# Eight buffers for the places of a group's rows, and block 1's experts on four column quarters with weights fetched early and the last choice's parts overlapped

## The chip, the cores and the metric

The kernel runs on one core of a Trainium2 chip. The metric is the device time of one execution in microseconds, the median of ten executions. The profiled execution is another one of the same program; its span goes from the first instruction to the last.

The engines are TensorE (PE, with its weight loads shown as PEld), VectorE (DVE), ScalarE (ACT), GpSimd (POOL) and SyncE (SP). SP, ACT and POOL issue DMA transfers; sixteen DMA engines carry them. A matmul of f32 stands in the profile as two MATMUL instructions, each with a weight load of its own; they are called passes here.

## The reference

The input is 32 images of 128 channels, 56x56 pixels, in f32. Two blocks follow each other. Block 0 is a depthwise 7x7 convolution, a layer norm over the channels and a mixture of eight experts, two for each of the 100,352 tokens, with a capacity for each expert. Block 1 takes the tokens of each image (3136) through an attention in which each token only attends within its own channels, head by head, and then through experts that choose tokens:

```python
logits = jnp.einsum('bsd,ed->bse', x, gate_w) + gate_b
probs = jax.nn.softmax(logits, axis=1)
vals, idx = jax.lax.top_k(probs.transpose(0, 2, 1), K)
...
pooled = jnp.einsum('bked,bke->bed', gathered, topv)
h = jnp.concatenate([pooled.transpose(1, 0, 2), ones], axis=-1)
h = jax.nn.gelu(jnp.einsum('ebd,edh->ebh', h, weight1), approximate=False)
h = jnp.concatenate([h, ones], axis=-1)
out = jnp.einsum('ebh,eho->ebo', h, weight2)
...
weighted = jnp.einsum('beo,bke->bkeo', out, topv).reshape(Bn, K * E, O)
outputs = outputs.at[jnp.arange(Bn)[:, None], flat_idx].add(weighted)
```

So each of the 64 experts sees one pooled row of 128 channels for each of the 32 images, takes it to 512 features (weight1, whose last row is a bias), through a Gelu and back to 128 channels (weight2, also with a bias row). The result goes back to the chosen tokens with the weights they were chosen with.

## The kernel before

**Stages.** One after the other: the convolution on PE (to `conv_d` in DRAM); routing of block 0's tokens; the choice of who keeps a place; the scatter of rows to their experts; block 0's experts; block 1's attention with the choices of its experts; block 1's experts; the output. Instructions are put in an order by the tile framework, which also inserts the waits and may move an instruction ahead of others on its engine; where `InOrder` wraps an engine (line 161, which all its instructions carry in the profile), the order of the text holds.

**Scatter (lines 659 to 810).** 112 groups of 896 tokens, seven tiles of 128 tokens each. In each turn of the loop `places(g)` has DVE write the row numbers of a group into `rd` (4 buffers, the pool's number), `rows(g)` builds the rows `xs` (6 buffers), and `send(g)`, two turns after `places`, has POOL issue seven indirect DMAs (line 697), which read `rd` and `xs`. A buffer of `rd` is free for DVE when the DMAs of the group four before have landed.

**Attention.** A loop over 784 tiles of 128 tokens, software-pipelined by hand. The 128x2048 tiles `s` (5 buffers) and `ev` (3) carry the scores and the weighted values of one tile each, 8 KB a partition. The pool `at` holds them and all else of the loop. Work of a group of seven tiles hangs at given places of the loop, and after every second image `choose(pr)` runs for a pair of images: the eight largest of 3136 for each expert and image (DVE), the exponentials (ACT), the chosen weights `pb`, stored to `mk_d` (SP), and then ten parts. A part transposes `pb` in tiles (PE, `cm`), scales them (ACT, `mT`), multiplies them with the normed tokens `u` (PE, `acc`) and adds the sum to `pT` (DVE). `choose` is a generator; each `yield` gives way to other work until the next half step. For the last pair there is no other work left.

**Block 1's experts (lines 1422 to 1486).** These open when the attention's pools are closed. `hbr` (biases of weight1) is fetched and turned, `pT` is turned to `pTb` (channels x experts x images, four matmuls of 512 columns, two PSUM buffers). Then 16 steps of four experts each. A step fetches `fw1` (1 MB, SP), `fw2` (four DMAs of 256 KB in rows of 512 bytes, ACT, line 1455) and the bias rows `fw2b` (SP); all three have 3 buffers. The products have weight1 as the stationary operand and 32 columns, one for each image, as the moving one, 16 matmuls `p_fh` a step (line 1463); DVE adds the bias, ACT applies the Gelu, and 16 matmuls `p_fo` (line 1480) with the 32 columns stationary and 128 columns of weight2 moving give 32 rows (images) by 4x128. DVE adds the bias row into `so`. After the last step `so` is stored to `fo_d` in one DMA (1 MB, line 1485) and read back as `outF` with the experts on the partitions (1 MB in rows of 512 bytes, line 1486), both on SP.

**Output (lines 1488 to 1500).** For each image SP fetches the chosen weights `mk` (784 KB, and 12 KB of `al`) and the tokens `to` (1568 KB), PE multiplies `outF` with `mk` in seven chunks of 448, DVE adds, and ACT stores 1568 KB. All tiles have 2 buffers.

Of the kernel before, what the change touches and what calls it, by code (L numbers as in the profile page):

```python
# [8 lines left out]
F32 = mybir.dt.float32  # L9
I32 = mybir.dt.int32  # L10
U32 = mybir.dt.uint32
AF = mybir.ActivationFunctionType
# [5 lines left out]
P = 128  # L18
# [7 lines left out]
def conv_attn_hybrid_kernel(  # L26
# [632 lines left out]
    with tc.tile_pool(name="sc_c", bufs=1) as cc, tc.tile_pool(  # L659
# [89 lines left out]
        def places(g):  # L749
# [5 lines left out]
            rds[g] = sc.tile([P, GJ], I32, name="rd")  # L755
# [169 lines left out]
    FAR = -3.0e38  # L925
    with tc.tile_pool(name="at_c", bufs=1) as cc, tc.tile_pool(
# [19 lines left out]
        wpr = at.tile([C, C], F32, name="wpr", tag="s", bufs=5)  # L946
# [3 lines left out]
        wpT = at.tile([C, C], F32, name="wpT", tag="ev", bufs=3)  # L950
# [142 lines left out]
        def offsets(n):  # L1093

            s = ss_[n] = at.tile(sh, F32, name="s", bufs=5)
# [17 lines left out]
        def values(n):  # L1113
            ev = evs[n] = at.tile(sh, F32, name="ev", bufs=3)
            kv = kvs[n - n % 2][:, n % 2]
            ve.tensor_tensor(ev, ss_[n], over_queries(kv[:, 1]), ALU.mult)
# [173 lines left out]
        def choose(pr):  # L1290
# [21 lines left out]
            yield  # L1312
            for im in range(2):
                e = slice(im * E2, (im + 1) * E2)
                parts = [(gl, *s[1:]) for gl in range(GPP) for s in tile_parts(gl) if s[0] == im]
                px = 0
                for gi, (gl, j0, j1, p) in enumerate(parts):
                    u, r = us[pr * GPP + gl]
                    pn, nj = p.stop - p.start, j1 - j0
                    ps = atp.tile([P, GJ, E2], F32, name="cm", tag="tp", bufs=3)  # L1320
                    for j in range(nj):
                        pe.transpose(
                            ps[:pn, j, :], pb[e, px + j * pn : px + (j + 1) * pn], ident[e, e]
                        )
                    px += nj * pn
                    yield
                    yield
                    mT = at.tile([P, GJ, E2], F32, name="mT", bufs=1)
                    if p.start:
                        sc.copy(mT[p, :nj], ps[:pn, :nj])  # L1330
                    for j in range(nj):
                        sc.activation(
                            mT[p, j], mT[p, j] if p.start else ps[p, j], AF.Copy,
                            scale=r[p, j0 + j : j0 + j + 1],
                        )
                    yield
                    yield
# [193 lines left out]
```

## Time and profile before

| | |
|---|---|
| median of ten runs | 9583.01 us (9570.92 to 9588.28) |
| profiled execution | 9579.16 us, span 9577.4 us, mean granted clock of PE 0.941 |
| busy: PE, DVE, ACT, POOL | 8686.7 (91%), 6480.8 (68%), 5266.6 (55%), 6772.9 us (71%) |
| DMA | 849.94 MB, mean 89 GB/s |

Stages by their place in the span: convolution to about 700 us, routing to 1050, keeping to 1320, scatter to 2330, block 0's experts to 4400, attention with its choices to 9018, block 1's experts to 9198, output to 9577.

In the lines below, a group of instructions is given as line, engine, operation, tile written and tiles read, shape, count, then busy time and the mean of one in ns, then the idle time before them and what ended it. A line of a window gives the busy time and count of each engine in a stretch of the span, the granted clock of PE as a share of full speed, the share in which the 16 DMA engines were busy, and GB/s. A line of the chain gives a start, a duration and what the time went to. Busy time of PE includes time in which a matmul is in the array at a lower clock.

### The profile page before, as it was taken

Reading aid. Unit: us, or ns where it says so; the run is one execution under the profiler, and the core shown is the slowest. Engines: PE = TensorE matmul, PEld = TensorE weight load, DVE = VectorE, ACT = ScalarE, POOL = GpSimd, SP = SyncE. Lnnn points to the kernel's source line nnn. Section 1 sums busy time; section 2 is a strip of 40 time slices with the busy share of each in tenths; the row PEclk is TensorE's granted clock in tenths of the full one; section 3 lists DMA queues with packets and bytes.
Section 4 is the critical chain, followed back from the end, with each engine's and each line's share of the span. In section 5 each row is a group of like instructions: output and inputs, shape, how many; then the busy total and the mean of one; then the engine's idle time right before and its main releaser. Section 6 shows DMA issues by size and latency. Waiting matters only on the chain. (4 is left out here: it accounts for less than half of the span.)

```text
span 9577.4 us, 165805 instructions
## 1 busy us (share of the span) xinstructions
PE 8686.7 (91%) x62536; PEld 7094.3 (74%) x62536; DVE 6480.8 (68%) x10965; ACT 5266.6 (55%) x13385; POOL 6772.9 (71%) x4884
## 2 busy tenths in 40 slices
PE   9999467776999999997999999999999999999888
PEld 4449445554766766666888998998988898898853
DVE  1127888885222222225999999999999999999423
ACT  1116633333333333335888888888888888888400
POOL 0002147776787777787999999999999999999300
PEclk9999789998999999999999999999999999999765
DMA  9995247775444444442000000000000000000389
GB/s 207 215 199 144 64 115 210 208 209 160 74 66 65 67 70 69 70 69 32 24 31 31 31 31 27 28 27 31 31 31 31 31 24 31 31 31 26 95 280 333
DMA packets 1019570, 849.94 MB, mean 89 GB/s; under 512 B 525876, under 2 KB 912247, under 8 KB 999250
## 3 DMA queue, kind: packets, MB, share of 16 engines
q1 hardware_dynamic: 464018, 479.57, 17.9%
q0 software_dynamic: 177664, 188.81, 11.4%
q10 hardware_dynamic: 377088, 170.96, 6.6%
q8 instruction: 495, 8.11, 0.4%
q14 instruction: 305, 2.50, 0.1%
HBM read 486.34 MB, written 353.64 MB: 88 GB/s over the span
## 5 line engine op out<-in xcount | busy, mean ns | idle before, releaser
L161 POOL TENSOR_TENSOR s<-s,q 128x2048 f32<-128x2048 f32 x784 | 3597.6, 4599 | 137.8 <-DVE s L161 106.7
L161 ACT ACTIVATE s<-s 128x2048 f32<-128x2048 f32 x784 | 1500.6, 1914 | 685.4 <-POOL s L161 682.5
L161 POOL DMA_INDIRECT t_d<-ys,xe x992 | 1530.7, 1543 | 412.0 <-issue 229.9
L161 DVE TENSOR_TENSOR s<-kv,c 128x2048 f32<-128x2048 f32 x784 | 1788.6, 2281 | 7.9 <-POOL c L161 7.6
L161 DVE TENSOR_TENSOR ev<-s,kv 128x2048 f32<-128x2048 f32 x784 | 1785.7, 2278 | 2.3 <-ACT s L161 2.2
L161 PE MATMUL sm<-ident,ev 128*128 128x128 f32 x12544 | 1534.3, 277 | 45.7 <-DVE ev L161 45.7
L161 PE MATMUL sm<-ident,s 128*128 128x128 f32 x12544 | 1525.2, 275 | 8.1 <-ACT s L161 8.1
L161 PEld LDWEIGHTS sm<-ident,ev 128*128 128x128 f32 x12544 | 1439.3, 144 | 93.2 <-DVE ev L161 50.8
L161 PEld LDWEIGHTS sm<-ident,s 128*128 128x128 f32 x12544 | 1403.1, 143 | 20.6 <-ACT s L161 8.5
L888 ACT ACTIVATE hT<-ph,b1t 128x512 f32<-128x512 f32 (+1 forms) x992 | 679.3, 685 | 1237.8 <-PE ph L884 1222.1
L899 DVE TENSOR_TENSOR ys<-py,b2t 128x512 f32<-128x512 f32 (+1 forms) x248 | 171.5, 691 | 1529.2 <-PE py L894 1427.4
L894 PEld LDWEIGHTS py<-w,hT 128*128 128x128 f32 x7936 | 958.0, 192 | 201.9 <-issue 91.4
L884 PE MATMUL ph<-xeT,w 128*128 128x512 f32 (+1 forms) x1984 | 921.6, 597 | 70.5 <-DVE xeT L880 70.5
L894 PE MATMUL py<-w,hT 128*128 128x128 f32 x7936 | 982.0, 277 | 0.1
L697 POOL DMA_INDIRECT xb_d<-xs,rd x784 | 766.2, 977 | 240.2 <-issue 203.2
L241 PE MATMUL cps<-xin,br 56*64 56x448 f32 x7168 | 686.1, 541 | 12.7 <-DVE br L235 11.0
L884 PEld LDWEIGHTS ph<-xeT,w 128*128 128x128 f32 x1984 | 348.8, 191 | 392.7 <-issue 292.8
L161 PE MATMUL pa<-rw,ct 128*128 128x256 f32 x1568 | 425.6, 416 | 202.4 <-DVE xs L161 202.4
L241 PEld LDWEIGHTS cps<-xin,br 56*64 56x64 f32 x7168 | 300.1, 133 | 398.1 <-issue 395.5
L161 PEld LDWEIGHTS pa<-rw,ct 128*128 128x128 f32 x1568 | 302.5, 205 | 335.0 <-DVE xs L161 247.1
L287 POOL MEMSET code<- 128x64 f32 x1 | 0.2, 151 | 695.2 <-DMA conv_d<-ot 695.2
L161 PE MATMUL kv<-wq,zT 128*128 128x256 f32 x1568 | 417.7, 390 | 54.4 <-DVE ev L161 54.1
(327 smaller groups left out, 13471.4 us busy)
## 6 DMA issues: line engine op xcount, KB each, us to landing
ct<-conv_d SPq DMA_DIRECT2D x192, 448.0 KB
xin<-in_x_dram SPq DMA_DIRECT2D x256, 196.0 KB
conv_d<-ot ACTq DMA_DIRECT2D x512, 98.0 KB
t_d<-xs ACTq DMA_DIRECT2D x112, 448.0 KB
tr<-t_d SPq DMA_DIRECT2D x112, 448.0 KB
to<-t_d SPq DMA_DIRECT2D x32, 1568.0 KB
out_dram<-oo ACTq DMA_DIRECT2D x32, 1568.0 KB
xg<-in_x_dram SPq DMA_DIRECT2D x96, 448.0 KB
```

The source lines that it names most:

```text
L161: r = getattr(self.engine, name)(*a, **k)
L241: nc.tensor.matmul(pss[r][b * HP : (b + 1) * HP], br[rows, kw, :], xi[rows, b * NB : (b + 1) * NB, kw : kw + W], start=(kw == 0), stop=(kw ...
L287: nc.gpsimd.memset(code, -1.0)
L697: s = nc.gpsimd.indirect_dma_start(out=xb_d, out_offset=bass.IndirectOffsetOnAxis(ap=idx, axis=0), in_=row, in_offset=None, bounds_check=R ...
L884: nc.tensor.matmul(ph[:, :, :rows], w1[:, f * P : (f + 1) * P], xT[:, :, :rows], start=True, stop=True,)
L888: nc.scalar.activation(hT[:, f, :, :rows], ph[:, :, :rows], AF.Gelu, bias=b1t[:, f : f + 1])
L894: nc.tensor.matmul(py[:rows, j, :], hT[:, f, j, :rows], w2[:, f, :], start=(f == 0), stop=(f == NF - 1),)
L899: nc.vector.tensor_tensor(ys[:rows], py[:rows], across(b2t, SB)[:rows], ALU.add)
```

## The change

**Places.** `rd` gets 8 buffers instead of 4.

**Pools.** A pool `big` is opened before the attention's pools and stays open to the end. The tiles `s` (5) and `ev` (3), and the two setup tiles that shared their buffers, move from `at` to `big`.

**Weights.** `fetch(i)` loads both weights of a step of four experts into these buffers: `fw1` into those of `s` (5), `fw2` into those of `ev` (3), each in one DMA of 1 MB on SP, and `fw2` with four consecutive rows of weight2 on a partition (2 KB in one piece). The first three steps are fetched in the loop's turn `NT + 4`, four turns after the last tile entered it and ahead of the last choice; the others inside the loop over steps.

**Last choice.** For the last pair of images the parts run in `in_turn_parts`: the next part's transposes are issued ahead of this part's sum, the parts of one image add up in PSUM (a `kv` buffer), and DVE copies the sum to `pT` once an image; `mT` takes the two buffers of `oT`. For other pairs nothing changes but that the code is cut into functions (`part_turned` is the scaling and `part_sum` the product, both as before).

**Experts.** The step's 32 columns of each expert become the stationary operand and weight1 the moving one, 512 columns; the four experts of a step stand on four column quarters of PE (`tile_position=(0, q * N)`), so that one PSUM bank holds 4x32 rows by 512. ACT copies it to SBUF, four transposes turn it back (each reads every fourth column, which fits the new order of weight2), DVE adds the bias while it empties PSUM, and the Gelu follows. The second product runs on column quarters as well, 16 matmuls of 128 columns, and its result and `so` have 128 rows (expert of the step, image). The bias rows of all steps are fetched once (`ob`, four DMAs). ACT stores each step's `so` to `fo_d`, and `outF` is read back in four DMAs of eight images each, on ACT's queue.

```diff
-            rds[g] = sc.tile([P, GJ], I32, name="rd")
+            rds[g] = sc.tile([P, GJ], I32, name="rd", bufs=8)
...
+    Q = 4
+    NS = E2 // Q
+    assert N * Q == P and 2 * NS <= 2 * E2
+
+    largest = ExitStack()
+    big = largest.enter_context(tc.tile_pool(name="big", bufs=1))
+    fw1s, fw2s = {}, {}
+
+    def fetch(i):
+
+        e = slice(i * Q, (i + 1) * Q)
+        fw1s[i] = big.tile([C, Q, FF2], F32, name="fw1", tag="s", bufs=5)
+        nc.sync.dma_start(fw1s[i], weight1[e, :C, :].rearrange("e c f -> c e f"))
+        fw2s[i] = big.tile([P, Q, NF2, C], F32, name="fw2", tag="ev", bufs=3)
+        nc.sync.dma_start(fw2s[i], weight2[e, :FF2, :].rearrange("e (p f) o -> p e f o", f=NF2))
...
-        wpr = at.tile([C, C], F32, name="wpr", tag="s", bufs=5)
+        wpr = big.tile([C, C], F32, name="wpr", tag="s", bufs=5)
...
-            s = ss_[n] = at.tile(sh, F32, name="s", bufs=5)
+            s = ss_[n] = big.tile(sh, F32, name="s", bufs=5)
...
-            ev = evs[n] = at.tile(sh, F32, name="ev", bufs=3)
+            ev = evs[n] = big.tile(sh, F32, name="ev", bufs=3)
...
+            if pr == N // 2 - 1:
+                yield from in_turn_parts(pr, pb, parts)
+                return
...
+        def part_turn(pb, part):
+            im, gl, j0, j1, p, px = part
+            e, pn = slice(im * E2, (im + 1) * E2), p.stop - p.start
+            ps = atp.tile([P, GJ, E2], F32, name="cm", tag="tp", bufs=3)
+            for j in range(j1 - j0):
+                pe.transpose(
+                    ps[:pn, j, :], pb[e, px + j * pn : px + (j + 1) * pn], ident[e, e]
+                )
+            return ps
...
+        def in_turn_parts(pr, pb, parts):
+
+
+            ahead = part_turn(pb, parts[0])
+            for i, part in enumerate(parts):
+                im, px = part[0], part[-1]
+                if px == 0:
+                    ps = atp.tile([P, E2], F32, name="acc", tag="kv", bufs=3)
+                mT = part_turned(pr, ahead, part, "oT", 2)
+                if i + 1 < len(parts):
+                    ahead = part_turn(pb, parts[i + 1])
+                done = i + 1 == len(parts) or parts[i + 1][0] != im
+                part_sum(pr, ps, mT, part, px == 0, done)
+                if done:
+                    ve.tensor_copy(pT[:, :, 2 * pr + im], ps)
+                yield
...
+            if k == NT + 4:
+                for i in range(3):
+                    fetch(i)
...
-            nc.tensor.transpose(ps[:, f, :], rows[:, f * P : (f + 1) * P], ident[:E2, :E2])
+            nc.tensor.transpose(ps[:, f, :], rows[:, f::NF2], ident[:E2, :E2])
...
+        ob = cc.tile([P, NS, C], F32, name="ob")
+        for q in range(Q):
+            nc.sync.dma_start(
+                ob[q * N : (q + 1) * N],
+                weight2[q::Q, FF2, :].partition_broadcast(N),
+            )
...
+        so = cc.tile([P, NS, C], F32, name="so")
+        for i in range(NS):
+            if i not in fw1s:
+                fetch(i)
+            w1, w2 = fw1s.pop(i), fw2s.pop(i)
+            ph = fps.tile([P, FF2], F32, name="p_fh", bufs=2)
             for q in range(Q):
-                nc.scalar.dma_start(
-                    w2[:, q], weight2[e0 + q, :FF2, :].rearrange("(f p) o -> p f o", p=P)
-                )
-            w2b = fp.tile([N, Q, C], F32, name="fw2b")
-            nc.sync.dma_start(w2b, weight2[e0 : e0 + Q, FF2, :].partition_broadcast(N))
-            ph = fps.tile([P, Q * NF2, N], F32, name="p_fh")
-            for q in range(Q):
-                for f in range(NF2):
+                nc.tensor.matmul(
+                    ph[q * N : (q + 1) * N], pTb[:, i * Q + q, :], w1[:, q, :],
+                    start=True, stop=True, tile_position=(0, q * N), skip_group_check=True,
+                )
+            h = fp.tile([P, FF2], F32, name="fh")
+            nc.scalar.copy(h, ph)
+            pt = fps.tile([P, NF2, P], F32, name="p_ft", tag="p_t", bufs=2)
+            for f in range(NF2):
+                nc.tensor.transpose(pt[:, f, :], h[:, f::NF2], ident)
+            hT = fp.tile([P, NF2, P], F32, name="fhT")
+            nc.vector.tensor_tensor(
+                hT.rearrange("p f (q n) -> p f q n", q=Q),
+                pt.rearrange("p f (q n) -> p f q n", q=Q),
+                hb[:, :, i * Q : (i + 1) * Q].unsqueeze(3).to_broadcast([P, NF2, Q, N]),
+                ALU.add,
+            )
+            nc.scalar.activation(hT, hT, AF.Gelu)
+            po = fps.tile([P, C], F32, name="p_fo", bufs=1)
+            for f in range(NF2):
+                for q in range(Q):
                     nc.tensor.matmul(
-                        ph[:, q * NF2 + f, :], w1[:, q, f * P : (f + 1) * P], pTb[:, e0 + q, :],
-                        start=True, stop=True,
+                        po[q * N : (q + 1) * N], hT[:, f, q * N : (q + 1) * N], w2[:, q, f, :],
+                        start=(f == 0), stop=(f == NF2 - 1), tile_position=(0, q * N),
+                        skip_group_check=True,
                     )
-            hT = fp.tile([P, Q * NF2, N], F32, name="fhT")
-            nc.vector.tensor_tensor(
-                hT.rearrange("p (q f) n -> p q f n", f=NF2),
-                ph.rearrange("p (q f) n -> p q f n", f=NF2),
-                hb[:, :, e0 : e0 + Q].rearrange("p f q -> p q f").unsqueeze(3).to_broadcast(
-                    [P, Q, NF2, N]
-                ),
-                ALU.add,
-            )
-            nc.scalar.activation(hT, hT, AF.Gelu)
-            po = fps.tile([N, Q, C], F32, name="p_fo")
-            for q in range(Q):
-                for f in range(NF2):
-                    nc.tensor.matmul(
-                        po[:, q, :], hT[:, q * NF2 + f, :], w2[:, q, f, :],
-                        start=(f == 0), stop=(f == NF2 - 1),
-                    )
-            nc.vector.tensor_tensor(so[:, e0 : e0 + Q, :], po, w2b, ALU.add)
-        nc.sync.dma_start(fo_d, so)
-        nc.sync.dma_start(outF[:E2], fo_d.rearrange("n e c -> e n c"))
+            nc.vector.tensor_tensor(so[:, i, :], po, ob[:, i, :], ALU.add)
+            nc.scalar.dma_start(
+                fo_d.rearrange("n (s q) c -> s q n c", q=Q)[i], so[:, i, :]
+            )
+        for n in range(0, N, N // 4):
+            nc.scalar.dma_start(
+                outF[:E2, n : n + N // 4, :], fo_d[n : n + N // 4].rearrange("n e c -> e n c")
+            )
```

## Prediction

> **What bounds the kernel now.** I read the page first, then the windows of the two places that the change touches, then the chain of waits and the groups by line there. On the page, POOL, DVE and PE are busy in turn over most of the span; a share of the whole says little here, so each stage is read for itself.
>
> The scatter stage (some 1325 to 2330 us), where the places are used, by groups of instructions on POOL:
>
> ```profile
> L697 POOL DMA_INDIRECT xb_d<-xs,rd x469 | 458.6, 978 | 142.9 <-issue 121.0 <-DVE xs L161 16.7 <-DMA xb_d<-xs,rd 4.0
> ```
>
> This is a window of 600 us: 458.6 us busy and 142.9 us between, 601.5 us together. POOL issues one indirect DMA each 1.28 us (0.98 and a gap of 0.30) without a hole. The waits of the same window name the one the new buffers concern:
>
> ```profile
> DVE rd L161 <- DMA xb_d<-xs,rd: 48.8, 34, 3.9
> ```
>
> DVE stands 48.8 us for a free place buffer, but in this window it is busy 80 to 85 us in each 100, and POOL never runs dry.
>
> The end of the kernel, as windows (stretch; PE, PEld, DVE, ACT, POOL busy with counts; granted clock; DMA share; GB/s). The rows are the last choice's sums, the start of the experts, the experts, the way of their output through memory, and the output loop:
>
> ```profile
> 8982.30:9018.00 35.70, 30.67 (x150) 27.81 (x150) 2.46 (x10) 11.54 (x51) 0.00 (x0) 0.50 0.11 46
> 9018.00:9028.00 10.00, 8.09 (x14) 3.28 (x14) 6.33 (x8) 0.00 (x0) 0.00 (x0) 0.50 0.93 279
> 9028.00:9181.00 153.00, 150.49 (x1025) 143.96 (x1023) 22.39 (x33) 11.35 (x17) 0.00 (x0) 0.75 0.82 231
> 9181.00:9198.40 17.40, 0.01 (x1) 0.01 (x1) 0.23 (x1) 0.00 (x0) 0.00 (x0) 0.63 0.91 213
> 9198.40:9577.40 379.00, 343.93 (x448) 145.83 (x448) 134.22 (x224) 0.00 (x0) 0.00 (x0) 0.50 0.94 327
> ```
>
> In the experts PE is busy 150.5 of 153 us at a clock of 0.75, while the DMA moves 231 GB/s: PE sets that stage. The output loop is the reverse: 327 GB/s at a DMA share of 0.94, so its 379 us are the transfers' and nothing in the change shortens them. The groups of the experts show what PE does:
>
> ```profile
> L1463 PE MATMUL p_fh<-pTb,fw 128*128 128x32 f32 x512 | 81.2, 331 | 0.0
> L1480 PE MATMUL p_fo<-fw,fhT 128*32 128x128 f32 x512 | 70.2, 309 | 2.0 <-ACT fhT L1476 2.0
> ```
>
> Each of the 16 steps of four experts costs (81.2 + 70.2) / 16 = 9.5 us of PE, in 64 passes (a matmul of f32 is two). The first kind streams 32 columns past a fresh 128x128 load: 159 ns a pass, most of it loading. The chain that ended last agrees, and shows the way through memory after it:
>
> ```profile
> 9122.78 16.37 PE p_fh L1463 x96
> 9139.16 13.21 PE p_fo L1480 x96
> ...
> 9181.26 6.47 DMA fo_d<-so
> 9187.74 10.61 DMA outF<-fo_d
> ```
>
> And before the experts, the last choice's parts, one after the other:
>
> ```profile
> 8987.00 0.95 PE cm L161 x7
> 8987.98 0.05 issue
> 8988.03 0.32 ACT mT L161
> 8988.35 0.04 issue
> 8988.40 3.25 PE acc L161 x14
> ```
>
> **The change part by part.** The profiled execution has a span of 9577.4 us; the median of the ten runs is 9583.0, so 5.6 us are added at the end.
>
> **Eight place buffers: 0 us.** The wait of 48.8 us per 600 moves off DVE, but POOL's 784 issues at 1.276 us stay. The work that hides it is POOL's own queue; had POOL holes, the most to win would be its gaps not put down to issue, 16.7 + 4.0 us per 600, 35 us in the stage. Those gaps are, however, the same 0.30 us that every issue has, so I take 0. A loss would need DVE running ahead to hurt POOL, whose beat did not change while DVE waited or worked: bounds -3 to +3.
>
> **The last choice: -4.5 us.** Ten parts now take PE 30.67 us of 35.7 at half clock; the rest is PE waiting some 0.4 us a part for the first ACT scaling (4.9 us of idle before the sums, released by ACT). With the next part's transposes placed ahead of the sum, only the first wait stays. The scalings are seven at 0.22 us, 1.54 us a part, under the 4.2 us of PE. The ten DVE additions become two copies; they were off the path (0.27 us each). Bounds: 0, and -17 if the clock rises: the same parts took 0.65 + 1.77 us instead of 1.0 + 3.25 at clock 1.00 near 8950 us. The clock stayed at 0.50 at 86% busy here, so I take it held.
>
> **Weights of three steps early: priced with the experts.** Six transfers of 1.05 MB wait for the last s and ev tiles, free near 8950 us. The DMA is nearly idle there (0.06 share, then 0.00), and 6.3 MB at 343 GB/s (the output loop from 9300 to 9500 us) are 18 us, done before the choice ends at 9018. On SP, the last stores of t2 and al (8957 to 8968) and the 1.6 MB of chosen weights (8982) are queued behind them, none needed before the output loop. Without that cover the 18 us would come back.
>
> **The experts, by step: 163.3 to 106 us.** The start stays: 10.2 us from the last sum (9017.9) to the first product (9028.1), for pT's turn, the biases and four copies. Then, of each step:
> - First product, 4 matmuls of 512 columns, two passes each. A 512-column pass took 0.94 us at half clock (p_b, x4 in 3.75) and 0.46 at full (the experts of block 0, 921.6 us by 1984). If four column quarters run at once: 1.9 or 0.9 us. In the first convolution four 64x64 quarters do: 7168 passes of 535 ns in 686 us, 96 ns each.
> - Copy by ACT 0.59 (u<-p_u, same shape). Four transposes back, 8 passes of 0.226 us at half clock (sm, 16 in 3.62) or 0.119 at full: 1.8 or 0.95. This work is new. Bias 0.69, Gelu 0.63, as now.
> - Second product, 16 matmuls of 128 columns, four at a time: 8 pass times, 1.8 or 0.95. Its addition 0.35 (between 0.28 for 128x64 and 0.42 for 128x256). Handovers at some 0.08, 0.5.
>
> PE: 5.5 us a step at half clock, 2.8 at full, instead of 9.5. The chain from copy to addition, if steps do not overlap: 6.4 or 4.7 us. ACT loses the 64 issues of w2 (median 0.62 us, with waits that held its Gelu up for 86 us); they go to SP as 16 of about 0.4 us, beside 16 of w1 as now, and SP loses 16 bias rows for 4 at the start. ACT gains a store a step, 0.4 us, which waits for the step's last addition with the next step's copy behind it: it can only make the chain hold. DMA: 2.10 MB a step at 328 GB/s (325 and 330 in the two stretches where PE drew it hardest, 9028 to 9047 and 9105 to 9123) is 6.4 us. The three limits lie close together, and none near 9.5.
>
> From the end of the choice: the three early steps begin at 10.2, the first second product ends near 19 and frees the first of three w2 buffers; SP has waited there with the DMA idle for about 10 us. 24 transfers of 3.2 us follow without a hole: 77 us, to 96; the last product and addition 2 us, 98. The first images' loads, up to 4.8 MB, take between 0 and 15 us of this, as now (two were there before the output began). Half of it: 106 us. Bounds: 93 (343 GB/s, no loads between) and 10.2 + 16 x 7.5 = 130 (nothing overlaps, a hole of 1 us a step for the buffer's return).
>
> Two pages of the Trainium skill speak against the new form. TensorEngine Tiling, Tiling Modes, says that a change of tiling mode drains TensorE; each step of the new form changes twice, from quarters to whole for the transposes and back, where today's never does. No row shows a drain's length, and the convolution kept one mode. SBUF — State Buffer, Specifications, says that reads want at least two hits in a 16-byte line; the transposes read h at every fourth f32, one hit a line. By contiguous rows a load is 0.143 us; were it twice that, the eight of a step would add 1.1 us, 18 over the stage where the chain binds, and the sum would be 9531. The time goes by the contiguous row, the nearest.
>
> **Output of the experts: 17.1 to 8.4 us.** One store of 1 MB (6.5 us) becomes sixteen, of which only the last is after the addition; the read (10.6 us, while a 1.6 MB load ran beside it) becomes four. The tail of the old read ran near 175 GB/s, 6.0 us for 1.05 MB; with 2.4 for the last small store: 8.4. SP no longer stands at the store, and loads pass it. Bounds: 17 (the new store lands as slowly) and 5 (only the first quarter is waited for).
>
> **Sum.** 9577.4 - 0 - 4.5 - (163.3 - 106) - (17.1 - 8.4) = 9506.9 us of span; with 5.6: 9512.5, say 9513.
>
> **The rivals.**
> *The steps run as chains.* ACT's issue keeps the order and half clock stays: 130 us instead of 106, 9537. For it: four engine handovers a step and short bursts, as where the clock stands at 0.50 today. Against: now two or three steps are held together (x96), and two buffers of each tile remain.
> *DMA alone, at a risen clock.* 93 us, 13 less in the choice than taken (-12 instead of -4.5 is enough): 9513 - 13 - 7.5 - 1.5 = 9491. For it: the choice without holes. Against: the experts held 0.75 even at 98% busy.
> *The quarters do not run side by side* (the other side). Then a step has 8 passes of 512 columns, 8 transposes, and 32 passes of 128. At a clock of 0.75: 5.1 + 1.2 + 4.9 = 11.2 us, 189 us with the start, and 9513 + 83 = 9596; at half clock 16.6 us, above 9650. It decides from 10.4 us a step on: (163.3 + 4.5 + 8.7 - 10.2) / 16. For it: here quarters have 128 rows and 32 columns, a form that no row shows. Against: the convolution's 96 ns.
> *It does not do what it says.* The weight transfers stay behind the pool's release, or a single queue paces the stage like now: 9583 less 4.5 and 8.7, 9570.
>
> **How the numbers follow.** Forecast (9500 to 9527) 0.46; chains 0.22; DMA alone 0.20; no effect in the experts 0.05; not side by side 0.07. Under 0.2%, 19 us, the measurement can't tell a change from none. Faster: the first three, 0.88; same: the fourth and a little of the last, 0.06; slower: the rest of the last, 0.06. The range takes in both neighbours with their bounds: 9480 (DMA alone, and the choice at -17 with a risen clock to its end) to 9552 (chains, and 15 us of the first images' loads on top).
>
> **What would show it.** In the changed kernel's windows: the scatter stage of unchanged length; the six early transfers before 8985 us; experts near 6 us a step with the DMA over 300 GB/s and PE well under full; p_o beginning near 9128 and lasting 379 us. I am wrong if the first products take more than 2 us a step, if SP's early waits hold up stores that attention's end needs, or if the moved tiles change attention's steady beat.

## The result, and the profile after

The changed kernel takes 9505.02 us (median of 8 runs, 9494.74 to 9508.75) against 9582.12 us for the kernel before (28 runs): a ratio of 0.9918, 95% interval 0.991 to 0.9927, so 77 us less. The profiled execution has a span of 9498.8 us, 78.6 less than before.

Where they went, stage by stage (us, both profiles):

| stage | before | after | difference |
|---|---|---|---|
| start to the first send of the scatter | 1341.3 | 1338.6 | -2.7 |
| scatter, first to last send | 1003.9 | 1004.8 | +0.9 |
| last send to the store of the last chosen weights | 6637.1 | 6630.5 | -6.6 |
| last choice | 35.7 | 29.7 | -6.0 |
| end of the choice to the experts' last addition | 163.3 | 99.6 | -63.7 |
| from there to the first product of the output | 17.2 | 16.1 | -1.1 |
| output loop | 379.0 | 379.6 | +0.6 |

The boundaries are read to some 0.3 us. The first row holds no changed work, and of the third only the pools and the early loads at its end are new. Both differ as much between the profiles of the changed kernel and its variants on this kind of chip: the first send lies between 1331.6 and 1348.3 us, and the third row between 6629.7 and 6637.9. Some 8 of the 78.6 us are therefore not to be put down to the change.

The windows that answer to those of before (stretch; PE, PEld, DVE, ACT, POOL; granted clock; DMA share; GB/s), first the last choice, then the start, the experts in four stretches, the way through memory and the output:

```profile
8973.90:9003.50 29.60, 29.15 (x150) 27.27 (x150) 0.27 (x1) 11.43 (x51) 0.00 (x0) 0.50 0.13 55
9003.50:9016.00 12.50, 7.42 (x16) 3.02 (x17) 6.58 (x8) 0.00 (x0) 0.00 (x0) 0.52 0.61 94
9016.00:9028.40 12.40, 11.71 (x155) 6.36 (x154) 4.34 (x8) 5.82 (x9) 0.00 (x0) 1.00 0.52 169
9028.40:9040.90 12.50, 6.24 (x114) 3.84 (x110) 2.26 (x5) 2.33 (x4) 0.00 (x0) 0.94 1.01 357
9040.90:9082.00 41.10, 26.71 (x276) 13.80 (x276) 5.90 (x12) 7.87 (x13) 0.00 (x0) 0.73 1.05 383
9082.00:9103.10 21.10, 12.16 (x164) 6.67 (x164) 3.64 (x7) 4.27 (x7) 0.00 (x0) 0.84 0.82 235
9103.10:9119.20 16.10, 0.00 (x0) 0.01 (x1) 0.29 (x1) 0.00 (x0) 0.00 (x0) 0.53 0.64 175
9119.20:9498.80 379.60, 342.95 (x448) 145.97 (x448) 134.29 (x224) 0.00 (x0) 0.00 (x0) 0.50 0.95 333
```

The experts have turned over: PE, busy 98% of the stage before, is busy 26.7 of 41.1 us in its middle, and the DMA moves 383 GB/s at a share of 1.05. The first 25 us behind the choice are the hole: 94 and 169 GB/s, since all eight buffers for weights are full and come free only when the first steps are done.

The groups of the experts, by instruction (the last number ahead of the arrow is the idle time before it):

```profile
L1521 PE MATMUL p_fh<-fw,pTb 128*32 128x512 f32 x128 | 25.5, 819 | 2.8 <-DMA fw<-in_L_ffn_weight_dram 2.8
L1541 PE MATMUL p_fo<-fw,fhT 128*32 128x128 f32 x512 | 22.9, 326 | 17.9 <-ACT fhT L1537 15.1 <-DMA fw<-in_L_ffn_weight_dram 2.8
L1529 PE MATMUL p_ft<-ident,fh 128*128 128x128 f32 x64 | 12.6, 319 | 9.5 <-ACT fh L1526 9.5
L1531 DVE TENSOR_TENSOR fhT<-p_ft,hb 128x512 f32<-128x512 f32 x16 | 11.1, 692 | 37.6 <-PE p_ft L1529 37.6
```

A mean of 819 ns, but 25.5 us for 128 passes, 0.20 us each: four passes are in the array together. PE has 61 us for the 16 steps, 3.8 a step, where it had 9.5. By these rows PE waits for ACT, as a chain of steps would; whether that chain or the transfers set the pace is a question for the runs. The end of the chain of waits (start, duration, what):

```profile
9080.87 16.97 DMA fw<-in_L_ffn_weight_dram
...
9101.98 1.12 PE p_fo L1541 x32
...
9103.45 11.78 DMA fo_d<-so
...
9115.30 3.79 DMA outF<-fo_d
...
9119.22 21.26 PE p_o L1565 x28
```

The last step's first weights take 16.97 us to land, of which PE waits 0.6, and its store of 64 KB takes 11.78 us. And the issues of SP:

```profile
8916.56 14.93 SPq L938 DMA_DIRECT2D fw<-in_L_ffn_weight_dram  x3
8932.87 9.18 SPq L940 DMA_DIRECT2D fw<-in_L_ffn_weight_dram  x3
8945.25 0.37 SPq L938 DMA_DIRECT2D fw<-in_L_ffn_weight_dram  x1
8949.52 0.39 SPq L938 DMA_DIRECT2D fw<-in_L_ffn_weight_dram  x1
...
9017.09 0.39 SPq L938 DMA_DIRECT2D fw<-in_L_ffn_weight_dram  x1
9023.76 4.62 SPq L940 DMA_DIRECT2D fw<-in_L_ffn_weight_dram  x3
...
9087.28 0.71 SPq L1558 DMA_DIRECT2D mk<-mk_d  x1
```

Eight transfers are early, not six: the framework also took the first weights of steps 3 and 4 ahead, for which buffers were free. The first image load stands behind the last weights and ahead of the last store.

### The profile page after: what moved, and what is told of

It is laid out like the page before. It is cut to its first block, busy times and chain, and to the rows that moved or that the text cites. A ratio compares the mean times of both kernels' runs of the same rounds, so it can differ in the third digit from the quotient of the medians.

```text
span 9498.8 us, 165321 instructions
## 1 busy us (share of the span) xinstructions
PE 8543.6 (90%) x62216; PEld 6974.1 (73%) x62216; DVE 6479.6 (68%) x10957; ACT 5277.5 (56%) x13401; POOL 6778.1 (71%) x4884
## 5 line engine op out<-in xcount | busy, mean ns | idle before, releaser
L241 PEld LDWEIGHTS cps<-xin,br 56*64 56x64 f32 x7168 | 343.1, 132 | 358.0 <-issue 313.5
L161 PE MATMUL pa<-rw,ct 128*128 128x256 f32 x1568 | 391.8, 391 | 133.5 <-DVE xs L161 133.5
L161 PEld LDWEIGHTS pa<-rw,ct 128*128 128x128 f32 x1568 | 281.0, 192 | 265.2 <-DVE xs L161 179.3
```

Source lines behind the costliest of these rows:

```text
L161: r = getattr(self.engine, name)(*a, **k)
L241: nc.tensor.matmul(pss[r][b * HP : (b + 1) * HP], br[rows, kw, :], xi[rows, b * NB : (b + 1) * NB, kw : kw + W], start=(kw == 0), stop=(kw ...
```

## The experiments

Two theories. *Transfers*: behind the choice the bytes set the time, and an order, a shorter chain or faster products are worth only what they save of the hole, the stretch of low GB/s above. *Chain*: each step's way from the first product over copy, transposes, bias and Gelu to the second product sets it. Beside them, one edit at a time is undone. Each run has five executions (x12_half_w2 four), timed beside the kernel before on the same chip. The first four ran on another chip, where the kernel before takes 10001.31 us; the scatter stage lasts 1419 us in these four profiles. Only ratios and stages of them are compared.

All runs, from the end of the last choice (pT's last copy, its start or its end, 0.3 us apart) on, in us; MB and GB/s are from the window to the end:

| run | last addition | first p_o | end | MB | GB/s | median, ratio to before |
|---|---|---|---|---|---|---|
| before | 163.3 | 180.5 | 559.4 | 166 | 297 | 9582.12 |
| after | 99.6 | 115.7 | 495.3 | 157.5 | 318 | 9505.02, 0.9918 [0.991, 0.9927] |
| x0_after | 102.0 | 115.6 | 496.2 | 157 | 317 | 9507.08, 0.9924 [0.9911, 0.9938] |
| x1_rd4 | 101.0 | 115.5 | 499.2 | 158 | 316 | 9914.58, 0.9911 [0.9897, 0.9924] |
| x2_late_weights | 99.9 | 117.3 | 506.5 | 157 | 312 | 9924.25, 0.9918 [0.9905, 0.9932] |
| x3_plain_parts | 99.0 | 112.6 | 499.2 | 158 | 316 | 9925.93, 0.9924 [0.9911, 0.9938] |
| x4_512 | 116.3 | 128.2 | 511.5 | 157.5 | 308 | 9929.88, 0.9927 [0.9914, 0.9941] |
| x5_quarter_by_quarter | 109.5 | 116.1 | 500.9 | 157 | 314 | 9508.12, 0.9927 [0.9913, 0.994] |
| x6_images_first | 116.6 | 123.3 | 505.4 | 158 | 312 | 9510.9, 0.9929 [0.9916, 0.9943] |
| x7_ahead | 96.2 | 108.8 | 493.5 | 157 | 319 | 9494.45, 0.9915 [0.9902, 0.9929] |
| x8_images_last | 105.0 | 111.7 | 496.2 | 157 | 317 | 9505.09, 0.9923 [0.9909, 0.9936] |
| x2b_late | 113.7 | 129.2 | 510.9 | 166 | 325 | 9524.35, 0.994 [0.9927, 0.9954] |
| x12_half_w2 | 77.0 | 89.3 | 468.4 | 149 | 318 | 9486.29, 0.9902 [0.9887, 0.9917] |
| x10_best | 97.1 | 110.1 | 490.8 | 157.5 | 321 | 9505.31, 0.9927 [0.9913, 0.9941] |

**Four place buffers again.**

```diff
-            rds[g] = sc.tile([P, GJ], I32, name="rd", bufs=8)
+            rds[g] = sc.tile([P, GJ], I32, name="rd")
```

> The changed kernel with the place buffers back at 4. Mine: POOL sets the scatter stage, so its 784 issues still take about 1005 us from the first (1338.6 to 2344.4 in the changed kernel, 1341.3 to 2346.1 before), DVE waits for places again (some 49 us in 600), and the time is that of the changed kernel, 9505 us within 5. Rival: the places gave part of the gain of the stages before the last choice, which begins 8.4 us earlier in the changed kernel's trace (8973.9 against 8982.3); then this run is near 9513 and its scatter stage longer than 1005 us.

The scatter lasts 1419.5 us with four buffers, and 1419.7 with eight in x2_late_weights on the same chip. There it is slower for another reason (last section); on the other kind of chip it lasts 1003.9 us with four (the kernel before) and 1004.7 to 1006.7 in all profiles with eight. The buffers are worth nothing on either. Where their wait went is seen in the waits of the changed kernel, 1600 to 2200 us (who waits for what: us, times, longest):

```profile
DVE xs L161 <- DMA xb_d<-xs,rd: 50.3, 58, 2.8
```

Before it was `rd`, 48.8 us; now DVE stands at `xs`, whose six buffers are read by the same DMAs.

**Plain parts in the last choice.** The branch to `in_turn_parts` is left out, so that the last pair's parts run as all others.

```diff
-            if pr == N // 2 - 1:
-                yield from in_turn_parts(pr, pb, parts)
-                return
```

> The changed kernel with the last pair's parts one after the other as before. Mine: from the first transpose to the last sum 35.5 us instead of 29.5, at the half clock in both; 9505 + 6 = 9511 us. Rival (the clock decides, not the holes): the clock leaves 0.50 in one of the two and the difference is 10 us or more; or the scheduler fills the holes with other work, and it is 0.

The choice in this run, and then in x1_rd4 on the same chip, which has the new parts:

```profile
9389.10:9425.00 35.90, 30.68 (x150) 27.81 (x150) 2.63 (x10) 11.57 (x51) 0.00 (x0) 0.50 0.11 45
```

```profile
9393.50:9423.10 29.60, 29.14 (x150) 27.27 (x150) 0.27 (x1) 11.47 (x51) 0.00 (x0) 0.50 0.13 55
```

6.3 us: PE's idle time falls from 5.2 to 0.5 us, and its busy time by 1.5, which no run explains. The clock stays at 0.50 in both, at 98% busy too. In the medians 6 us can't be told from nothing.

**Late weights, by place in the text.**

```diff
-            if k == NT + 4:
-                for i in range(3):
-                    fetch(i)
```

> The changed kernel without the three early fetches; every weight is fetched after the last choice. Two theories of what paces the experts. By the chain of engines (6.2 us a step in the changed kernel's trace, one step behind the other): the first product waits some 6 us for its weights, then 16 steps of 6.2 follow, last addition some 109 to 115 us after the choice's end instead of 99.6; 9515 to 9520 us. By the transfers (385 GB/s in the middle of the changed kernel's experts): 33.5 MB are 87 us without a hole, and with the last step's chain some 97 us, so nothing is lost: 9500 to 9507 us.

It doesn't do what it says. SP in this run, whose choice ends at 9419.1:

```profile
9332.09 14.96 SPq L938 DMA_DIRECT2D fw<-in_L_ffn_weight_dram  x3
9348.43 9.18 SPq L940 DMA_DIRECT2D fw<-in_L_ffn_weight_dram  x3
```

The buffers of `big` are free and nothing else holds the loads, so the framework took them ahead although the text has them behind the choice. The call in the loop isn't what makes the weights early; that it is the pool that stays open fits, but no run closes it. So the loads were held by data.

**Late weights, held by the data.** For the first five `fw1` and three `fw2` DVE copies `pT`'s last column, one element a partition, into the buffer before its load.

```diff
+        if i < 5:
+            nc.vector.tensor_copy(fw1s[i][:, 0, :1], pT[:, 0, N - 1 :])
         nc.sync.dma_start(fw1s[i], weight1[e, :C, :].rearrange("e c f -> c e f"))
...
+        if i < 3:
+            nc.vector.tensor_copy(fw2s[i][:, 0, 0, :1], pT[:, 0, N - 1 :])
```

> Late weights, this time held by the data: one element of each of the first eight buffers is copied from the last column of pT, so that none of their loads can start before the choice is over. 8.4 MB more then move behind the choice. Transfers set the time: 8.4 MB at 340 GB/s is 25 us, of which some 15 fit into the hole that the changed kernel leaves there (12.2 us at 96 GB/s and 12.4 us at 169, 5.1 MB less than at 340): 502 to 512 us from the choice's end to the end, 9510 to 9530. The prediction's way, without a hole to fill: 25 us more, 9530. The order of products sets it: only the first load is waited for, some 6 us, and the steps keep their 6.4: 499 to 502, 9508 to 9512. Early weights do nothing: 9500 to 9508, as the run that only moved them in the text.

9524.35, and its runs (9520.86 to 9535.35) all lie above those of x0_after (9498.60 to 9510.74) on the same chip: 17 us in the medians. In the profiles it is 14.7 us between the choice and the end; another 22.0 lie ahead of that, in stages that the two kernels share, and aren't put down to the edit. The start and the experts, in windows of this run:

```profile
9022.70:9040.20 17.50, 6.29 (x12) 2.51 (x12) 7.61 (x17) 0.00 (x0) 0.00 (x0) 0.70 0.73 184
9040.20:9060.00 19.80, 12.96 (x112) 6.21 (x116) 2.66 (x5) 4.93 (x7) 0.00 (x0) 0.67 1.05 389
```

8.4 MB more move behind the choice. At 340 GB/s they are 25 us; the hole takes up ten of them: from 17.5 to 37.3 us behind the choice the DMA moves 389 GB/s, where it moves 283 in the first profile of the changed kernel and 302 in x0_after. That is the transfers' account of the start, and it says what early weights are worth here, 15 to 17 us.

**Half of the second weights.** Odd steps use the `fw2` of the step before. This run was to part the theories: the chain of a step is unchanged, the bytes are not.

```diff
+        if i % 2:
+            fw2s[i] = fw2s[i - 1]
+            return
         fw2s[i] = big.tile([P, Q, NF2, C], F32, name="fw2", tag="ev", bufs=3)
```

> Every second group of four experts uses the second weights of the group before it, whose loads are left out (8 of 32 transfers, 8.4 MB; all products are still made). Transfers set the experts' stage: 8.4 MB at 340 to 380 GB/s is 22 to 25 us less; last addition 75 to 80 us after the choice's end (99.6 now), 9478 to 9488 in all. The steps' chain of products, copies and transposes (6.1 to 6.5 us one after the other) sets it: last addition still at 95 to 101, 9498 to 9508. Both lie close together: the stage falls to the chain and stops there, about 90 to 95, 9493 to 9500.

The last addition comes at 77.0 us, 25 earlier than in x0_after. That is the number of the transfers' theory, but not its way, as the steps one by one show. The sum of a step is DVE's addition into `so`; its starts are in us from the choice's end, PE's waits for weights are those of both products in the whole stage, and the clock is the granted one from the seventh sum to the last:

| run | seventh sum | last sum | a step between | PE's waits for weights | clock |
|---|---|---|---|---|---|
| x12_half_w2 | 32.3 | 77.1 | 4.98 | 0 | 1.00 |
| after | 44.8 | 99.6 | 6.10 | 5.6 | 0.80 |
| x2b_late | 59.5 | 113.8 | 6.03 | 7.5 | 0.80 |
| x2_late_weights | 44.3 | 99.9 | 6.17 | 4.5 | 0.75 |
| x1_rd4 | 43.3 | 101.0 | 6.41 | 4.3 | 0.68 |
| x0_after | 43.4 | 102.2 | 6.54 | 4.0 | 0.65 |
| x5_quarter_by_quarter | 48.1 | 109.5 | 6.82 | 0 | 0.92 |
| x4_512 | 44.2 | 116.3 | 8.02 | 15.5 | 0.64 |
| x7_ahead | 40.8 | 96.2 | 6.15 | 22.9 | 0.67 |
| x10_best | 43.1 | 97.4 | 6.04 | 29.3 | 0.78 |

The bytes decide how soon the seventh sum comes: 32.3 us with fewer, 43.4 with all, 59.5 with eight more transfers behind the choice. From there on, in the first six rows, PE waits at most 0.6 us for weights, and the same chain takes 4.98 us a step at a clock of 1.00 and up to 6.54 at 0.65. The chain of waits of the changed kernel over such a step, and then that of x12_half_w2:

```profile
9046.25 1.93 PE p_fo L1541 x32
9048.18 1.68 PE p_fh L1521 x8
...
9049.88 0.59 ACT fh L1526
...
9050.52 0.77 PE p_ft L1529 x4
...
9051.37 0.70 DVE fhT L1531
...
9052.10 0.64 ACT fhT L1537
...
9052.78 1.79 PE p_fo L1541 x32
```

```profile
9054.59 1.08 PE p_fo L1544 x32
9055.67 0.89 PE p_fh L1524 x6
...
9056.64 0.59 ACT fh L1529
...
9057.28 0.76 PE p_ft L1532 x4
...
9058.14 0.70 DVE fhT L1534
...
9058.86 0.64 ACT fhT L1540
...
9059.55 1.12 PE p_fo L1544 x32
```

From product to product it is 6.5 us and 5.0: ACT and DVE take the same time in both, PE's products less in the second. So of the 25 us some 11 are won before the seventh sum, by the bytes, and 14 behind it, by nine steps at a higher clock. A DMA share near 1.00 doesn't show otherwise: x12_half_w2 has it too while PE waits for no weights at all.

```profile
9032.00:9065.00 33.00, 24.03 (x365) 13.47 (x364) 7.87 (x16) 9.51 (x16) 0.00 (x0) 1.00 1.00 365
```

Neither theory holds alone: the transfers set the start, and then the chain the steps, at the clock that is granted. Why the clock is higher in this run isn't shown; no run changes the clock alone.

**The second product quarter by quarter.** The two loops change places, so that consecutive passes lie on one quarter.

```diff
-            for f in range(NF2):
-                for q in range(Q):
+            for q in range(Q):
+                for f in range(NF2):
```

> The changed kernel with the second product's 16 matmuls ordered quarter by quarter (four sums of one expert, then the next expert), so that neighbours stand on the same quarter. Mine: the product's 32 passes take 1.1 us at full and 1.95 at half clock in the changed kernel because four quarters run at once; in this order they take about four times as long (3.5 to 7 us), the step's chain grows from 6.2 to 9 to 11, and the time to 9540 to 9575 us. Rival: the passes are paced by their issue or their weight loads and not by quarters side by side; then the order changes nothing, 9505 us.

```profile
L1541 PE MATMUL p_fo<-fw,fhT 128*32 128x128 f32 x512 | 45.0, 303 | 15.6 <-ACT fhT L1537 15.1 <-issue 0.4
L1521 PE MATMUL p_fh<-fw,pTb 128*32 128x512 f32 x128 | 23.6, 618 | 0.0
```

45.0 us where it was 22.9: the quarters do run side by side, and the order of issue decides how far. At full clock it is some 2.5 us a step (9064.0 to 9066.5) against 1.12, about twice and not four times. PE waits for no weights here, only for ACT, so the chain sets the stage: the last addition comes 7.5 us later than in x0_after. That the whole is only 4.7 us longer (500.9 behind the choice) owes to two things that the edit didn't aim at: a clock of 0.92 instead of 0.65 in the last nine steps, and a last store of 2.41 us instead of 9.41.

**Rows of 512 bytes for weight2,** as the kernel before read them. This needs four transfers a step instead of one, so two things change together.

```diff
-        nc.sync.dma_start(fw2s[i], weight2[e, :FF2, :].rearrange("e (p f) o -> p e f o", f=NF2))
+        for q in range(Q):
+            nc.sync.dma_start(
+                fw2s[i][:, q], weight2[i * Q + q, :FF2, :].rearrange("(f p) o -> p f o", p=P)
+            )
...
-                nc.tensor.transpose(pt[:, f, :], h[:, f::NF2], ident)
+                nc.tensor.transpose(pt[:, f, :], h[:, f * P : (f + 1) * P], ident)
```

> The changed kernel with weight2 as before: rows of 512 bytes, four fetches a step on SP, and the transposes read h and the biases in contiguous columns. Mine: the 2 KB pieces are why the experts' transfers run at 357 to 398 GB/s instead of the 328 that I took from the old mix; with 512 bytes the middle of the stage falls to some 325 to 340 GB/s, 6.3 us a step and 13 steps: 5 to 12 us longer, 9510 to 9517 us. The strided read costs nothing: a weight load of the transposes stays at 0.14 us at full clock and about 0.21 in the mean. Rival: the rate is set by what PE consumes (a step per 6.2 us), the time stays at 9505; or the strided read costs and contiguous columns shorten the loads to two thirds or less.

Last addition at 116.3, 15 us later than in x1_rd4 on the same chip. A window of its middle:

```profile
9455.00:9520.00 65.00, 38.53 (x410) 19.58 (x407) 8.85 (x18) 10.25 (x17) 0.00 (x0) 0.65 0.95 291
```

The DMA engines are nearly as busy as in the changed kernel (0.95 against 1.05), but move 291 GB/s instead of 383: 306 against 365 for each full share. A stretch at the same place in x1_rd4 (9450 to 9515) has 362 GB/s at 1.03. So this form of the loads costs bytes per time, and here the transfers do bind: PE's waits for weights rise from 4.3 to 15.5 us. How much of the 15 us is due to the four issues, and to SP's longer waits, wasn't tried apart.

**The images' loads first, and last.** Two runs on the slow store. In the one, SP loads the first two images before the experts' weights; in the other the text has ACT issue these loads behind the reads of `outF`:

```diff
+        images = {n: image(n) for n in range(2)}
         outF = cc.tile([E2 + 1, N, C], F32, name="outF")
```

```diff
         for n in range(N):
+            ld = nc.scalar if n < 2 else nc.sync
...
-            nc.sync.dma_start(mk[:E2], mk_d[n])
+            ld.dma_start(mk[:E2], mk_d[n])
```

> The changed kernel with the first two images' loads (4.7 MB) issued at the head of the experts, where the DMA moves 50 to 230 GB/s until the first w2 buffer is free (20 us after the choice). Mine: these loads stood in front of the last weights (a w1 took 17.0 us to land) and of the last store of so (11.8 us for 64 KB); moved, the last addition comes 5 to 8 us earlier, the store lands in 2 to 3 us, p_o begins 12 to 18 us earlier: 9488 to 9494 us. Rival: the store takes its 11.8 us whatever else moves, and the loads only delay other weights: 9500 to 9507 us.

> The changed kernel with the first two images' loads issued on ACT's queue behind the read of outF. Mine: the last store of so lands in 2 to 3 us instead of 11.8 and outF is there 6 us later, the last weights come 5 us earlier; p_o then waits for its first image, 2.4 MB or 7 us behind outF: about even, 9500 to 9508 us. Rival (the store is slow by itself): the store still takes over 10 us, and with the loads behind it 9512 to 9520 us.

The last store in x6_images_first, then in x8_images_last:

```profile
9118.99 2.41 DMA fo_d<-so
9121.57 3.83 DMA outF<-fo_d
```

```profile
9106.69 2.41 DMA fo_d<-so
9109.27 3.75 DMA outF<-fo_d
```

2.41 us in both. But x8_images_last doesn't do what it says: its choice ends at 9001.4, and ACT's queue has the first image's loads right there, the second's from 9015.28 on:

```profile
9001.44 0.56 ACTq L1559 DMA_DIRECT2D mk<-mk_d  x1
...
9002.74 0.35 ACTq L1562 DMA_DIRECT2D to<-t_d  x1
```

So in both runs the loads are early, and none has them last. The question of the store is answered all the same. It takes 11.78 us in the first profile, where the last image load went out 2.7 us ahead of it, 9.41 in x0_after (2.5 us ahead), and 2.41 in these two and in x5_quarter_by_quarter, where it was 8.9 us ahead. Nothing is gained: the loads delay the weights (in x6_images_first the first `fw2` behind the choice goes out at 9033.34 and the last addition comes at 116.6; in x8_images_last PE waits 19.0 us for weights and the last addition comes at 105.0), and the output loop takes 382.1 and 384.5 us instead of 379.6. The expectation of a gain was wrong for x6_images_first, 505.4 us behind the choice against 495.3. For x8_images_last about even was expected and came, 496.2, but not by the way that was meant.

**The next step's first product ahead, and an earlier start.** In x7_ahead PE's order is written out; x10_best also moves the fills of `outF` from DVE to POOL, since they stood 3.4 us ahead of `back`.

```diff
+        hT = turned_back(0, product(0))
+        for i in range(NS):
+            h = product(i + 1) if i + 1 < NS else None
+            second(i, hT)
+            hT = turned_back(i + 1, h) if i + 1 < NS else None
```

```diff
-        nc.vector.memset(outF[E2 : E2 + 1, :, : C - 1], -root / (1.0 - root))
+        nc.gpsimd.memset(outF[E2 : E2 + 1, :, : C - 1], -root / (1.0 - root))
```

> The changed kernel with PE's order written out: a step's first product goes ahead of the second product of the step before, and its transposes behind it. Chain theory: PE's order made each step 6.2 us of waits in turn; now PE has some 3.5 us a step, the transfers set 5.4 us, the last addition comes 8 to 12 us earlier: 9493 to 9497 us. Transfer theory: the DMA is at its share of 1.0 from 9028 to 9090 already, the steps cannot come faster: within 3 us of 9505.

> TensorE takes the next group's first product ahead of this group's second, as in the run before, and the two fills of outF go from VectorE to GpSimd, so that the turn of the sums starts 3.4 us earlier. The chain sets the stage: both add up, last addition 91 to 94 us after the choice's end (96.2 with the order alone), 9488 to 9494. Transfers set it: the earlier start is waited away at the next weights, 95 to 97, the end of the choice to the end 491 to 496, 9492 to 9500.

Each shortens the stage by a few us (96.2 and 97.1). In both PE now waits for weights, 22.9 and 29.3 us, and a step is hardly shorter (6.15 and 6.04 us): with the chain's waits filled, the transfers bind, so the two limits lie close together. The earlier start of x10_best, 9.5 us instead of 11 to 12.5, is lost again in this waiting. x10_best's whole and x7_ahead's are 490.8 and 493.5 us, the shortest with all the work.

The median of x7_ahead is the lowest with all the work, 9494.45. That lies in the range named for the chain, and the last addition between the two theories; but its interval overlaps with the changed kernel's. x10_best's, 9505.31, missed both expectations. Its profile lost 12 us before the choice's end, in stages it shares with x0_after (9012.8 against 9000.7). Whether either beats the changed kernel stays open.

**The changed kernel once more.**

> The changed kernel itself, as a measure of what two profiles of one kernel differ by, and beside it the three that follow. 9495 to 9512 us. If transfers alone set the time behind the choice, its end to the end of the span is 493 to 498 us again (495.3 in the first profile). If the 64 KB store of the last sums is slow because the image loads stand in front of it, it takes over 8 us again before the outF reads start (11.8); if that was chance, 2 to 5.

It repeats: 496.2 us, and a slow store again. One thing doesn't: PE's clock in the middle of the experts is 0.58 (9040.9 to 9082) where the first profile has 0.73, and the stage takes 102.0 instead of 99.6 us, for its chain goes at 6.54 us a step instead of 6.10.

## Why the prediction was right, point by point

The time was forecast at 9513 and is 9505; the sum gave a span of 9506.9 against 9498.8. That PE would no longer set the experts' stage held, and so did the shorter choice; what sets the stage instead was half right, and the closeness is partly luck: the terms missed by -6.4 (experts), +7.7 (their output), -1.5 (choice) and +0.6 (output loop), which nearly cancel, and 8.4 us less lie ahead of the last choice, within what the profiles differ by.

**Place buffers, 0.** Right (x1_rd4, and the scatter's length on both chips). The reason given, that POOL's own queue paces the stage, fits the unchanged rows on the chip of the forecast; DVE's wait only changed its name.

**Last choice, -4.5.** -6.0 here and -6.3 undone. Mechanism right: the idle time went, 4.7 us, and the clock did not rise. The 1.5 us of busy time that went too were not foreseen.

**Early weights.** They lay where the forecast put them, ahead of the choice's end, and the hole came too: the forecast has the first `fw2` buffer free at 19 us, SP issued its load at 20.3. Their price was left inside the stage's sum; x2b_late gives it, 15 to 17 us.

**Experts, 106.** 99.6 and 102.0. The step that failed here is that the transfers "follow without a hole" to 96 us. They set the time up to the seventh sum; behind it PE waits at most 0.6 us for weights, and nine steps of the chain, 6.1 to 6.5 us each, fill the other 55 to 59 us. The forecast had this chain among its limits, and said that they lie close together; where the transfers do bind, in x7_ahead, the last addition comes at 96.2, so that both ways lead near the forecast is luck. Mis-sized is the term "Half of it", 8 us for the images' loads: on SP they stand behind the last weights, at 9087.28, and the stage ends 1.6 to 4 us past the 98 that the forecast had without them. The rate was taken too low for the middle, 328 where 383 came (354 in x0_after); half of the old bytes were in rows of 512 bytes, which x4_512 shows to be slower together with four times the issues. The slow start gave that back. The transposes were counted as two passes each and are one (64 instructions for 64 transposes).

**The two rules.** The Trainium skill's page SBUF — State Buffer, Specifications, wants two hits in each 16-byte line of a read, and the forecast priced a miss at 0.143 us a load. Half of that is there: with contiguous rows (x4_512) a load's median is 142 ns, at every fourth f32 210. Four loads a step are 0.27 us, of which 0.1 is on the path: at full clock the four transposes take 0.75 us instead of 0.66. That a change of tiling mode drains TensorE (the skill's TensorEngine Tiling, Tiling Modes) has a price that no run here shows by itself; the four transposes after it took 0.75 us in all, of which a load and a pass alone are 0.49.

**Output of the experts, 8.4.** This is the step that failed: 16.1. It took "2.4 for the last small store", and 2.41 is what it takes alone; but the image loads that SP, no longer held up, put ahead of it made it 11.78. The forecast named these loads ("loads pass it") as a gain. The upper bound, 17, held. What the failure cost seems little: in x5_quarter_by_quarter and x8_images_last, with the fast store, the output loop takes 384.7 and 384.5 us instead of 379.6. No run shows the store alone.

**The rivals.** Chains at 130 us: fallen as priced, at 7.5 us for every step; but its mechanism, steps one after the other, is there in the last nine, at 6.1 to 6.5 us and clocks of 0.65 to 0.80. Transfers alone, 9491: right for the start, without the hole, the chain and the slow store, and the clock in the choice did not rise. Quarters not side by side: fallen, and their order is worth a factor of two in PE's time. No run undoes the quarters themselves; that they pay is read from PE's 3.8 us a step instead of 9.5. No effect in the experts: fallen.

## What to carry to other kernels

Taking bytes away shortened the stage by 25 us, and still that doesn't show the bytes to set its pace: look where in the stage the time went, step by step, with the waits and the clock beside it (x12_half_w2). A DMA share near 1.00 doesn't show it either. In a chain of short steps the granted clock is a term of its own, 4.98 us a step at 1.00 and 6.54 at 0.65. Where two limits lie close, an edit to one is worth little before the other binds (x7_ahead). And a load is early when its buffer is free and its data ready, not where the text has it.

## What was not expected

The clock in the experts differs between profiles of one kernel: 0.58 and 0.73 in the middle, and 1.00 in x12_half_w2, where PE is busy 73% of the middle instead of 65%. The two runs in which PE waits for no weights have 1.00 and 0.92 in the last nine steps, the others of the table 0.64 to 0.80. The Trainium skill has such a cause in TensorE: Matmul & The Clock Gate, HAM oscillation: waits for data, past some 3.4 us, let the clock fall between bursts. These runs agree in part: the longest wait of PE for weights in the first profile is 2.2 us, and x0_after waits less than it in all, at the lower clock. By the same page (What's actually happening) it rises after a busy window of 3.4 us; but here the last choice ran 29.6 us at 98% busy and a clock of 0.50, with matmuls of 64 columns and transposes, and there the measurement decides.

A store of 64 KB takes 2.41 us or 4.5 to 12 as the last one, by what is ahead of it on the DMA engines. And two chips differ by 415 us in one stage: the scatter takes 1419 us on the one, 1004 on the other, with the same instructions; there POOL waits 178 us in each 600 for DVE's `xs`, and the profile puts DVE's wait down to something outside the core's records.
